# Layer 0: the selection matrix first in its step, and sets 0 to 2 in five steps per two pairs instead of six

## The chip, the cores and the metric

The kernel runs on one core of a Trainium2 chip. Its time is the device time of one execution in microseconds (us); a profiled execution also gives a trace of all engines: PE (matmuls), PEld (its weight loads), DVE (vector), ACT (scalar, activations), POOL (GpSimd) and SP, whose queue issues most transfers.

## The reference

Four graph layers follow one another, each as `x = layernorm(x + layer(x, adj))`, over 128 graphs of 64 nodes with 128 features; all is float32. The change lies in the first, which is a continuous filter: for each of the 64 x 64 possible edges of a graph a distance d is spread over 20 Gaussians, run through a two-layer filter, weighed by a cutoff and summed over the neighbours.

```python
coeff = -0.5 / (widths * widths)
f_ij = jnp.exp(coeff * diff * diff)                 # diff = d_ij - offsets, 20 of them
rcut = 0.5 * (jnp.cos(d_ij * (math.pi / CUTOFF)) + 1.0) * (d_ij < CUTOFF)
y = x @ w_in2f
W = ssp(f_ij @ fw1 + fb1) @ fw2 + fb2               # ssp(v) = softplus(v) - log 2
W = W * rcut[..., None]
agg = jnp.einsum('bjf,bijf->bif', y, W)
out = ssp(agg @ ow1 + ob1) @ ow2 + ob2
```

The second layer is of the same kind with 64 Gaussians; the third and fourth are graph convolutions with the normalized adjacency.

## The kernel before

**Slots.** About a quarter of the edges are there, so the kernel does not compute 64 x 64 of them. A compaction picks the edges of each graph and stores them in DRAM as slots: a distance (d), the neighbour's number (j) and a weight (w). Graphs are sorted by size and taken in pairs, 64 pairs a layer; eight pairs form a set, and all pairs of a set have the same number of slots per graph (`GSLOTS`: 1080, 1092, 1044, 1020, 1008, 1008, 996, 948 in layer 0). Pair n of the loop runs over both layers, 0 to 127.

**Steps.** Two pairs (n and n + 1, n even) are cut into steps. `chunks_of` gives the cuts: in layer 1 wide cuts of 2/5 of a pair, whose two narrow middle ones `steps_of` joins into one step that holds the end of one pair and the start of the next (five steps); in layer 0 two cuts a pair up to 1024 slots (sets 3 to 7, four steps per two pairs) and three above (sets 0 to 2, six steps of 360, 364 or 348 columns). A step works on both graphs of a pair at once.

**What a step is.** The loop over `steps` writes out the order of all engines by hand, and nothing reorders it. With c the step, c1 and c2 the two before it:

- `sums` (DVE): the reductions over the slots of the previous two pairs' m, line 1931 and 1935, in eight parts; `TURNS[beat]["sums"]` says how many parts in each step
- `early`, `side`, `stores`: compaction of later sets (DVE's Max and index, lines 1259 and 1262; POOL's scatters, line 997; SP's loads of rows, line 1019), so many pieces a step; `early` gives 9 in the first 18 steps
- loads (SP, line 1381) of d for pair n + 2 or n + 3; three buffers hold d, three w, two j
- where a pair starts in the step: its `one_hot` (DVE, line 1822), the selection matrix, which writes w where the slot's neighbour number equals the row and zero elsewhere; also, now and then, work for a group of four pairs
- `filter_in(c)`: px, the first filter matmul (PE, line 1846), then Exp on ACT into h. In layer 0 d lies in three thirds on 20 rows each, so a cut over the border of a third needs a matmul more
- `gather(c1)`: pg, the neighbours' features by the selection matrix (PE, line 1875), copied by ACT into m (two buffers)
- the loads of j and w (SP)
- `softplus(c)`: Ln on ACT; then, at two places per two pairs, a set's sine if one is due (ACT, with a load of function tables before and after)
- `filter_out(c2)`: pw, the second filter matmul (PE, line 1861), then `message(c2)`: DVE multiplies pw into m (line 1901)
- `gaussians`: Square and Exp on d of a coming pair (ACT, line 957)

px, pg and pw have one PSUM buffer each. `slot(nodes)` and `slot(befores)` put the work per group of four pairs in between (u, o, back, xT, y, zT, zs on PE).

`TURNS` holds these counts by the number of steps per two pairs (6, 4 and 5, the last for layer 1), `BEFORES` the steps in which `befores` runs.

Of the kernel before, what the change touches and what calls it, by code (L numbers as in the profile page):

```python
# [66 lines left out]

def chunks_of(layer, size):

    if layer == 1:  # L70
        wide = -(-2 * size // 5)
        return (wide, wide, size - 2 * wide, size - 2 * wide, wide, wide)
    n = 2 if size <= 1024 else 3
    return (size // n,) * (2 * n)
# [538 lines left out]
def sparse_stack(ctx: ExitStack, tc: tile.TileContext, t: dict, out: bass.AP, flag):  # L613
# [801 lines left out]
    side, again0, sines = deque(), [], deque()  # L1415
# [400 lines left out]
    def one_hot(n):  # L1816

        _, j, wt = slot_data[n]
        layer, p = pair_at(n)
        size = GSLOTS[layer][p // 8]  # L1820
        hots[n] = wt
        nc.vector.scalar_tensor_tensor(  # L1822
            hots[n][:, 0:size], j[:, 0:size], near, wt[:, 0:size], ALU.is_equal, ALU.mult
        )
# [118 lines left out]
    befores, nodes, convs, sums = deque(), deque(), (deque(), deque(), deque()), deque()  # L1943
# [5 lines left out]
    messages, aggs, phase = {}, {}, [0]  # L1949
# [20 lines left out]
    N = 2 * NP  # L1970
# [12 lines left out]
    early = deque([gathering()])  # L1983
# [33 lines left out]
    def steps_of(n):  # L2017


        layer, p = pair_at(n)  # L2020
        size = GSLOTS[layer][p // 8]
        cuts, at = [], 0
        for m in CHUNKS[layer][p // 8]:
            cuts.append([part_of(n + at // size, at % size, at % size + m)])
            at += m
        if layer == 1:
            cuts[2:4] = [cuts[2] + cuts[3]]
        for k, cut in enumerate(cuts):
            yield dict(
                id=f"{n}_{k}", layer=layer, w=layers[layer], n=n, k=k, beat=len(cuts), parts=cut,  # L2030
                phase=k + p // 2 % 2 * len(cuts),
                size=sum(x["cols"][1] - x["cols"][0] for x in cut),
                starts=[x["n"] for x in cut if x["cols"][0] == 0],
            )
# [12 lines left out]
            late=(2, None, None, 3, None, None), load=(2, None, None, 3, None, None),  # L2047
            gauss=((1, 0), (1, 1), None, (2, 0), (2, 1), None),
            end=(7,) * 6,
        ),  # L2050
        4: dict(
            sums=(2, 3, 2, 2), early=(6, 7, 6, 7), side=(2, 3) * 2,
            late=(2, None, 3, None), load=(2, None, 3, None),
# [10 lines left out]
    FREE, MORE, ONCE, FAST = 4, 4, 1, (0, 0)  # L2064
    SUMS = (2, 2, 3, 4, 4)
    EARLY = {N - gap: q for gap, q in zip((14, 11, 8), small_groups)}
    BEFORES = {6: (3, 4, 7, 8, 9), 4: (2, 3, 5, 6, 7), 5: (7, 8, 9)}

    block = nc.cur_bb.bb.instructions
    past = [None] * 2  # L2070
# [1 line left out]
    for i in range(len(steps) + 2):  # L2072
        c, c1, c2 = steps[i] if i < len(steps) else None, *past
        now = c or dict(steps[-1], k=i - len(steps), phase=i - len(steps), starts=[])
        n, k, beat, layer = now["n"], now["k"], now["beat"], now["layer"]
        turn = {name: values[k] for name, values in TURNS[beat].items()}
        phase[0], at_step[0] = now["phase"] if n < N - FREE else None, i

        if n >= N - 2:
            run(sums, SUMS[k] if c is not None else 9)  # L2080
        else:
            run(sums, turn["sums"])
        run(early, 9 if i < 18 else turn["early" if n < NP - 8 else "end"])
        for _ in range(turn["side"] // 2):
            run(side, min(2, len(side)))
        if turn["side"] % 2:
            run(side, min(1, len(side)))
        run(stores, 1)
        if NP + 5 in now["starts"]:
            assert not early and not side and not convs[0], "edges are still to be gathered"  # L2090
            compacting.close()
            rings.append(ctx.enter_context(tc.tile_pool(name="srings", bufs=4)))
            for q in (0, 1, *small_groups):
                group = GROUPS[1][q]
                blocks[q] = rings[0].tile(
                    [P, group.stop - group.start, P], F32, name=f"blocks{q}", bufs=1
                )
                nc.gpsimd.memset(blocks[q], 0.0)

            small[2] = by_pair(node.tile([P, GS * P], F32, tag="zt", name="small2", bufs=1))  # L2100
            small[3] = zblk
        if c is not None:
            if turn["load"] is not None and n + turn["load"] < N:
                m = n + turn["load"]
                if len(c["parts"]) == 1:
                    slot_data[m], late_loads[m] = later_loads(m)
            for part_ in c["parts"]:
                m, (_, q) = part_["n"], part_["at"]
                if part_["cols"][0] > 0:
                    continue  # L2110
                if m + GS < N:
                    ahead(m)
                if part_["s"] == min(1, len(range(NP)[GROUPS[layer][q]]) - 1):
                    load_nodes(layer, q)
                if m > 0:
                    one_hot(m)
                if m in EARLY:
                    last[EARLY[m]].append(normals_of(EARLY[m]))
            filter_in(c)
            if len(c["parts"]) == 2 and n + 3 < N:  # L2120
                slot_data[n + 3], late_loads[n + 3] = later_loads(n + 3)
        if c1 is not None:
            gather(c1)
        if c is not None and turn["late"] is not None and n + turn["late"] < N:
            late_loads.pop(n + turn["late"])()
        if layer == 1 and befores and (n >= N - 8 or phase[0] in BEFORES[beat]):
            slot(befores)
        if c is not None:
            softplus(c)
            if beat % 2 == 0 and k % (beat // 2) == beat // 2 - 1 and sines:  # L2130

                sines.popleft()()
        if layer == 0:
            slot(nodes)
            if befores and phase[0] in BEFORES[beat]:
                slot(befores)
        if n >= N - MORE:
            slot(nodes)
            if not ONCE:
                slot(convs[2])  # L2140
        if N - FAST[0] <= n < N - FAST[1]:
            slot(convs[1])
        if c2 is not None:
            filter_out(c2)
        for queue in last.values():
            slot(queue)
        if layer == 1:
            slot(nodes)
        if c2 is not None:
            message(c2)  # L2150
        if convs[0]:
            slot(convs[0])
        if n >= N - MORE:
            slot(convs[2])
        if c is not None and turn["gauss"] is not None:
            m, stage = n + turn["gauss"][0], turn["gauss"][1]
            for stage in range(begun.get(m, 0), stage + 1 if m < N else 0):
                gaussians(m, stage)
                begun[m] = stage + 1
        slot(convs[1])  # L2160
        for queue in last.values():
            slot(queue)
        past = [c, c1]
# [70 lines left out]
```

## Time and profile before

| | us |
|---|---|
| median of 3 runs | 1550.03 |
| lowest and highest | 1546.11, 1555.68 |
| the profiled execution | 1555.04 |
| its span | 1553.2 |

The mean granted clock of PE was 0.986. Where the span goes, by the shapes of ACT's Exp in the timeline: sets 0 to 2 of layer 0 from 69.7 to 339.8 us, sets 3 to 7 to 726 us, layer 1 with the two convolutions behind that. What each step takes from one Exp to the next is some 2.7 to 3.7 us in sets 0 to 2 where nothing else comes between, and 4.0 to 4.7 in sets 3 to 7.

A line of the profile names an engine, a line of the program, an operation, what is written from what, the shape and how many there are; after a bar come the busy time and the mean of one in ns, and after another the idle time of the engine before them and what ended it.

### The profile page before, as it was taken

To read this page: it belongs to the slowest core of one execution; us is meant where nothing else is said; L and a number is where in the kernel's file an instruction comes from. 1 tells how busy PE (TensorE), PEld (TensorE's weight loads), DVE (VectorE), ACT (ScalarE), POOL (GpSimd) and SP (SyncE) were. 2 spreads that over 40 slices of the span, in tenths; PEclk is the share of its full clock that TensorE was granted. 3 is DMA by queue.
4 is the path that set the end of the run, shared out by engine and by line. 5 is a ranking of instruction groups with operands and counts; after the bars stand their busy time and mean duration, and the time that the engine had idled before them with its cause. 6 is when DMAs were issued, how large, how long until landed. Compare 5 with 4: busy or idle time off the path is not lost.

```text
span 1553.2 us, 23194 instructions
## 1 busy us (share of the span) xinstructions
PE 1418.0 (91%) x6841; PEld 786.0 (51%) x6841; DVE 1320.7 (85%) x2919; ACT 1316.4 (85%) x1659; POOL 730.6 (47%) x1139
## 2 busy tenths in 40 slices
PE   1388999999989999999999999999999999999975
PEld 1144455544444444555444555555555555555454
DVE  8798889888989899878888888888888888888886
ACT  1368798989888989989999999999999999999853
POOL 2433445545574545424822235554456555464422
PEclk9999999999999999999999999999999999999997
DMA  6856454656554645446666556555555555555201
GB/s 208 260 129 147 115 133 117 138 129 137 134 130 125 146 126 124 125 126 147 155 161 157 135 121 152 132 140 129 135 146 132 135 138 133 120 140 140 65 1 30
DMA packets 122280, 205.60 MB, mean 132 GB/s; under 512 B 47956, under 2 KB 80034, under 8 KB 121506
## 3 DMA queue, kind: packets, MB, share of 16 engines
q1 hardware_dynamic: 113330, 188.40, 49.3%
q0 software_dynamic: 6576, 14.99, 2.9%
q8 instruction: 57, 0.93, 0.3%
q10 hardware_dynamic: 2240, 0.65, 0.2%
q14 instruction: 77, 0.63, 0.1%
HBM read 185.29 MB, written 18.64 MB: 131 GB/s over the span
## 4 chain that ended last, share of the span: by engine, by line
PE 62%; DVE 12%; ACT 10%; DMA 5%; issue 4%; SPq 3%; POOL 0%; DVEq 0%; ACTq 0%
PE pw L1861 23%; PE px L1846 13%; PE pg L1875 11%; ACT h L957 4%; DVE m L1901 3%; SPq L1381 2%; DMA w<-w_dram 2%; PE y L1507 2%; DVE agg L1931 2%; DVE w L1822 1%; PE o L1648 1%; PE hw L1738 1%; PE u L1631 1%; PE back L1657 1%; ACT d L957 1%
## 5 line engine op out<-in xcount | busy, mean ns | idle before, releaser
L957 ACT ACTIVATE h<-h,half 128x1008 f32<-128x1008 f32 (+12 forms) x313 | 332.7, 1063 | 0.1
L957 ACT ACTIVATE m<-pg 128x1008 f32<-128x1008 f32 (+12 forms) x313 | 291.9, 933 | 42.1 <-DVE agg L1935 20.6
L1875 PE MATMUL pg<-w,ys 64*128 64x504 f32 (+15 forms) x1376 | 298.5, 517 | 21.7 <-issue 7.4
L1861 PE MATMUL pw<-h,w_L_gnn_W2T 128*128 128x504 f32 (+8 forms) x640 | 296.8, 586 | 1.8 <-DVE m L1901 1.5
L1931 DVE TENSOR_REDUCE agg<-m 128x32 f32<-128x544 f32 (+14 forms) x455 | 287.3, 669 | 1.8 <-PE u L1631 0.4
L1901 DVE SCALAR_TENSOR_TENSOR m<-pw,c_L_gnn_b,m 128x1008 f32<-128x1008 f32 (+8 forms) x161 | 194.8, 1210 | 106.3 <-PE pw L1861 92.8
L1861 PE MATMUL pw<-h,w_L_gnn_fw 128*128 128x504 f32 (+6 forms) x608 | 252.8, 538 | 8.4 <-DVE m L1901 6.3
L1901 DVE SCALAR_TENSOR_TENSOR m<-pw,c_L_gnn_fb,m 128x1008 f32<-128x1008 f32 (+6 forms) x152 | 168.9, 1111 | 70.1 <-PE pw L1861 51.9
L957 ACT ACTIVATE h<-px,c_L_gnn_b 128x1008 f32<-128x1008 f32 (+8 forms) x160 | 171.5, 1072 | 28.0 <-PE px L1846 27.9
L1822 DVE SCALAR_TENSOR_TENSOR w<-j,row,w 128x1212 f32<-128x1212 bf16 (+12 forms) x128 | 182.4, 1425 | 6.0 <-DMA w<-w_dram 6.0
L957 ACT ACTIVATE h<-px,c_L_gnn_fb 128x1008 f32<-128x1008 f32 (+6 forms) x152 | 148.2, 975 | 45.6 <-PE px L1846 39.2
L1875 PEld LDWEIGHTS pg<-w,ys 64*128 64x128 f32 x1376 | 128.0, 187 | 112.7 <-issue 52.5
L1861 PEld LDWEIGHTS pw<-h,w_L_gnn_W2T 128*128 128x128 f32 x640 | 108.7, 189 | 150.0 <-issue 79.1
L1846 PE MATMUL px<-d,fw 64*128 64x168 f32 (+10 forms) x928 | 154.0, 437 | 25.6 <-ACT d L957 18.7
L1846 PE MATMUL px<-d,w1t 64*128 64x504 f32 (+11 forms) x768 | 172.7, 540 | 0.5 <-ACT h L957 0.4
L1861 PEld LDWEIGHTS pw<-h,w_L_gnn_fw 128*128 128x128 f32 x608 | 105.0, 193 | 90.1 <-issue 43.3
L1846 PEld LDWEIGHTS px<-d,fw 64*128 64x128 f32 x928 | 73.6, 187 | 125.5 <-ACT h L957 33.1
L1476 POOL TENSOR_SCALAR rs<-mv 128x4 f32<-128x4 f32 x55 | 13.9, 253 | 251.4 <-DVE mv L1469 250.4
L957 ACT ACTIVATE d<-d,neg_off 128x1212 f32<-128x1212 f32 (+12 forms) x128 | 120.8, 944 | 9.0 <-DMA d<-d_dram 9.0
L997 POOL DMA_INDIRECT rows<-comb,goes x64 | 72.4, 1131 | 91.8 <-DMA rows<-comb,goes 68.1
L997 POOL DMA_INDIRECT out_dram<-gz,at_row x56 | 72.9, 1302 | 76.2 <-DMA out_dram<-gz,at_row 51.0
L1482 POOL TENSOR_SCALAR x_all<-ny,mv,rs 128x128 f32<-128x128 f32 x120 | 106.3, 894 | 3.2
(333 smaller groups left out, 2280.4 us busy)
## 6 DMA issues: line engine op xcount, KB each, us to landing
d<-d_dram SPq DMA_DIRECT2D x32, 315.0 KB
w<-w_dram SPq DMA_DIRECT2D x32, 315.0 KB
d<-d_dram SPq DMA_DIRECT2D x32, 303.0 KB
w<-w_dram SPq DMA_DIRECT2D x32, 303.0 KB
w<-w_dram SPq DMA_DIRECT2D x32, 252.0 KB
j<-j_dram SPq DMA_DIRECT2D x32, 157.5 KB
j<-j_dram SPq DMA_DIRECT2D x32, 151.5 KB
d<-d_dram SPq DMA_DIRECT2D x16, 300.0 KB
```

The source lines that it names most:

```text
L957: latest = nc.scalar.activation(out_, in_, func, **kw)
L997: nc.gpsimd.indirect_dma_start(out=into, out_offset=bass.IndirectOffsetOnAxis(ap=at, axis=0), in_=rows, in_offset=None,)
L1381: engine.dma_start(to, dram_ap(slots[layer, name][s], first, [[0, to.shape[0]], [1, n]]))
L1482: (nc.gpsimd if apart else nc.vector).tensor_scalar(dst[:, s, :], y[:, s, :], mv[:, s, 0:1], rstd[:, s : s + 1], ALU.subtract, ALU.mult,)
L1507: nc.tensor.matmul(ps[:, s, :], lhsT=xt[:, s * P : (s + 1) * P], rhs=w["win"], start=True, stop=True)
L1631: nc.tensor.matmul(by[:, s, :], lhsT=w["o1"], rhs=of, start=layer == 1, stop=True)
L1822: nc.vector.scalar_tensor_tensor(hots[n][:, 0:size], j[:, 0:size], near, wt[:, 0:size], ALU.is_equal, ALU.mult)
L1846: nc.tensor.matmul(ps[:, b, at : at + m], lhsT=w["w1"][rows, :] if c["layer"] else w["w1"][rows, k, :], rhs=d[rows, col : col + m], start= ...
L1861: nc.tensor.matmul(c["pw"][:, b, :], lhsT=c["w"]["w2"], rhs=c["h"][:, b, :], start=True, stop=True)
L1875: nc.tensor.matmul(ps[:, b, to], lhsT=y[rows, :], rhs=hots[part_["n"]][rows, first:stop], start=True, stop=True,)
L1901: nc.vector.scalar_tensor_tensor(to, c["pw"][:, :, of], c["w"]["b2"], to, ALU.add, ALU.mult)
L1931: nc.vector.tensor_reduce(av[:, :, :, r], both, AX.X, ALU.add)
```

## The change

`chunks_of` cuts layer 0's sets above 1024 slots as layer 1's, and `steps_of` joins the middle cuts wherever there are six. Two pairs of sets 0, 1 and 2 are then five steps of 432, 437 or 436, 418 or 416 columns. They get counts of their own, `TURNS[3]` and `BEFORES[3]`. In all of layer 0 `one_hot` moves from behind the sums and the compaction to the start of the step. The places of the sine are written anew: steps 2 and 4 of five (2 and 5 of six before), 1 and 3 of four as before.

```diff
-    if layer == 1:
+    if layer == 1 or size > 1024:
         wide = -(-2 * size // 5)
         return (wide, wide, size - 2 * wide, size - 2 * wide, wide, wide)
...
-        if layer == 1:
+        if len(cuts) == 6 and (True):
             cuts[2:4] = [cuts[2] + cuts[3]]
...
+        3: dict(
+            sums=(2, 2, 1, 2, 2), early=(5, 6, 5, 6, 6), side=(2, 2, 3, 2, 3),
+            late=(2, None, None, 3, None), load=(2, None, 3, None, None),
+            gauss=((1, 1), None, (2, 0), (2, 1), (3, 0)),
+            end=(7,) * 5,
+        ),
...
-    BEFORES = {6: (3, 4, 7, 8, 9), 4: (2, 3, 5, 6, 7), 5: (7, 8, 9)}
+    BEFORES = {6: (3, 4, 7, 8, 9), 4: (2, 3, 5, 6, 7), 5: (7, 8, 9), 3: (3, 4, 6, 7, 8)}
...
-        turn = {name: values[k] for name, values in TURNS[beat].items()}
+        turns = TURNS[3 if layer == 0 and beat == 5 else beat]
+        turn = {name: values[k] for name, values in turns.items()}
         phase[0], at_step[0] = now["phase"] if n < N - FREE else None, i
 
+        for m in now["starts"] if layer == 0 else ():
+            if m > 0:
+                one_hot(m)
         if n >= N - 2:
             run(sums, SUMS[k] if c is not None else 9)
...
-                if m > 0:
+                if m > 0 and layer == 1:
                     one_hot(m)
...
-            if beat % 2 == 0 and k % (beat // 2) == beat // 2 - 1 and sines:
+            if layer == 0 and k in (beat // 2 - (beat != 5), beat - 1) and sines:
```

For the counts of before: six steps had `sums=(1, 1, 2, 1, 2, 2)`, `early` 2, 5, 5, 2, 5, 5, `side` 2 in each, d of pairs n + 2 and n + 3 loaded in steps 0 and 3, j and w likewise, and the Gaussians as (pair, stage) (1, 0), (1, 1), none, (2, 0), (2, 1), none.

More of the change, by code (lines that the diff above doesn't have):

```diff
@@ L2125, in sparse_stack @@
             late_loads.pop(n + turn["late"])()
-        if layer == 1 and befores and (n >= N - 8 or phase[0] in BEFORES[beat]):
+        if layer == 1 and befores and (n >= N - 8 or phase[0] in BEFORES[3 if layer == 0 and beat == 5 else beat]):
             slot(befores)
@@ L2134, in sparse_stack @@
             slot(nodes)
-            if befores and phase[0] in BEFORES[beat]:
+            if befores and phase[0] in BEFORES[3 if layer == 0 and beat == 5 else beat]:
                 slot(befores)
```

## The prediction

> **What bounds the kernel now.** I read the page first: busy shares, then the chain of work that ended last.
>
> ```profile
> PE 1418.0 (91%) x6841; PEld 786.0 (51%) x6841; DVE 1320.7 (85%) x2919; ACT 1316.4 (85%) x1659; POOL 730.6 (47%) x1139
> PE 62%; DVE 12%; ACT 10%; DMA 5%; issue 4%; SPq 3%; POOL 0%; DVEq 0%; ACTq 0%
> ```
>
> PE leads with 91% and carries 62% of the chain; DVE and ACT stand just behind, and 8% is transfers and their queue. An average says little of a change to one stage, so next come the windows by stage. The shapes of ACT's Exp (h<-px) give the limits: sets 0 to 2 (720, 728, 696 elements, that is two halves of 360, 364, 348 columns) run from 69.7 to 339.8 us, the rest of layer 0 (four wide steps) to 726. "Double pair" below means two pairs, as the step loop takes them: 12 of them lie in sets 0 to 2.
>
> ```profile
> 164.00:339.80 175.80, 165.00 (x808) 90.67 (x804) 152.59 (x404) 151.09 (x219) 93.27 (x146) 0.99 0.54 128
> 339.80:579.90 240.10, 224.92 (x1090) 115.57 (x1088) 218.17 (x608) 207.24 (x255) 133.06 (x225) 0.99 0.54 131
> 579.90:726.00 146.10, 144.59 (x743) 77.28 (x740) 122.90 (x226) 133.45 (x167) 55.36 (x96) 1.00 0.53 132
> ```
>
> Columns: length, then busy time of PE, PEld, DVE, ACT, POOL, the granted clock, DMA share, GB/s. Sets 1 and 2 (8 double pairs, six steps each): 22.0 us per double pair, PE idle 10.8 us or 1.35 each. Sets 3 to 5 (12, four steps): 20.0 us, PE idle 15.2 or 1.27 each. Sets 6 and 7, with little compaction left: idle 1.5 in all, 0.19 each. So PE sets the pace everywhere, its idle time goes with the compaction on DVE, POOL and SP, and hardly with the number of steps.
>
> Then PE's timeline, one undisturbed step of each kind:
>
> ```profile
> 215.62 0.88 PE L1846 MATMUL px<-d,fw 64*128 64x364 f32 x4
> 216.33 0.78 PE L1875 MATMUL pg<-w,ys 64*128 64x364 f32 x4
> 217.04 1.49 PE L1861 MATMUL pw<-h,w_L_gnn_fw 128*128 128x364 f32 x4
> 218.46 0.88 PE L1846 MATMUL px<-d,fw 64*128 64x364 f32 x4
> ...
> 517.26 1.12 PE L1846 MATMUL px<-d,fw 64*128 64x336 f32 x8
> 518.21 1.01 PE L1875 MATMUL pg<-w,ys 64*128 64x504 f32 x4
> 519.16 1.96 PE L1861 MATMUL pw<-h,w_L_gnn_fw 128*128 128x504 f32 x4
> 521.04 1.12 PE L1846 MATMUL px<-d,fw 64*128 64x168 f32 x8
> ```
>
> From px to the next px: 2.84 us at 364 columns, 3.78 at 504. Slope (3.78 - 2.84) / 140 = 6.7 ns a column; what no column explains is 2.84 - 364 x 0.0067 = 0.40 us a step.
>
> **The change part by part.** *One step less per double pair, on PE.* The columns stay (2160, 2184, 2088), the 0.40 goes once: 12 x 0.40 = -4.8 us. The stage rows check it: PE's busy time per double pair is 20.6 against 18.7 us; of the 1.9 the 112 columns explain 0.75, the other 1.1 is two steps, 0.57 each, so -6.8. I take -4.8, the row of steps that are like those changed.
>
> *More pieces in the first matmul.* Cuts of 432 no longer fall on the thirds of 360: 10 pieces per double pair in place of 6, two of them 72 wide (73 and 70 in sets 1 and 2). The 336+168 step above takes 0.95 from px to pg, as long as the 504 pg behind it (0.95), so pieces down to 168 are free. For 72 the bounds are 0.84 ns a column (0.306 us from one 364-wide record to the next), 0.061, and the nearest row, the 128-wide matmuls, 0.111 apart: 0 to 0.05 each, two passes, two pieces, 12 times, so 0 to +2.4 us. I take +2.4. [...]
>
> *ACT and DVE.* Each step has an Exp, a copy and a Ln on ACT:
>
> ```profile
> L957 ACT ACTIVATE h<-h,half 128x728 f32<-128x728 f32 x24 | 21.7, 902 | 0.0
> L957 ACT ACTIVATE h<-px,c_L_gnn_fb 128x728 f32<-128x728 f32 x24 | 20.8, 867 | 7.7 <-PE px L1846 7.6
> L957 ACT ACTIVATE m<-pg 128x728 f32<-128x728 f32 x24 | 18.6, 773 | 3.0 <-PE pg L1875 2.7 <-issue 0.2
> ...
> L957 ACT ACTIVATE h<-h,half 128x1008 f32<-128x1008 f32 x32 | 36.3, 1133 | 0.0
> L957 ACT ACTIVATE h<-px,c_L_gnn_fb 128x1008 f32<-128x1008 f32 x32 | 35.0, 1092 | 10.0 <-PE px L1846 9.4 <-issue 0.4
> L957 ACT ACTIVATE m<-pg 128x1008 f32<-128x1008 f32 x31 | 31.2, 1006 | 12.6 <-DVE agg L1935 5.1 <-PE pg L1875 4.1 <-issue 3.4
> ```
>
> Lines through the two sizes leave fixed parts of 0.30, 0.28 and 0.17: 0.75 us a step, 9.0 in all. DVE's message (971 ns at 728, 1261 at 1008) leaves 0.22, 2.6 in all. ACT idles 24.7 of 175.8 us, waiting mostly for PE, so these are hidden behind PE but for their shares of the chain (10% and 12%): -0.9 and -0.3. [...]
>
> *A tighter wait.* The sums of a double pair are eight parts. With six steps (1, 1, 2, 1, 2, 2) the last is done in step 0 of the double pair after next, with five (2, 2, 1, 2, 2) in step 1, the very step in which ACT's copy reuses that m buffer and, every second time, PE starts u. Four-step sets stand so already: ACT waited there for agg L1935 11.7 us in 20 double pairs, 0.58 each. 12 x 0.58 = 7 us of ACT, which its 24.7 us of idle covers; behind the waiting copy are Ln and the next Exp, and PE after those. At nothing; +7 if the cover is gone.
>
> *Compaction earlier.* A double pair now advances it by 28 pieces in place of 24 (by 45 in place of 54 in the first 18 steps, 9 each). In the order of instructions 250 of its DVE instructions, not 229, lie in the first 12 double pairs; at about 0.25 us (0.21 to 0.29 for Max and index) 5 us are moved ahead and missing later. DVE idles 23 us in each of the two stages: nothing. The sine (0.41 us and two table loads of 1.28) comes once a set as before.
>
> *Loads.* d is read two steps after its load, not three (2 x 4.35 = 8.7 us for 3 x 3.65 = 10.9), j and w of a second pair four, not six (17.4 for 22). The tightest pair I found:
>
> ```profile
> 264.90 2.31 SPq L1381 DMA_DIRECT2D d<-d_dram  x6
> 271.40 0.60 SPq L1381 DMA_DIRECT2D w<-w_dram  x1
> 274.74 0.58 ACT L957 ACTIVATE d<-d,neg_off 128x348 f32<-128x348 f32 x1
> 284.20 1.30 DVE L1822 SCALAR_TENSOR_TENSOR w<-j,row,w 128x1044 f32<-128x1044 bf16 x1
> ...
> 108.01 4.96 DMA w<-w_dram
> ```
>
> d has 7.5 us from the last issue to its use, 5.3 after the change; the chain shows landings of 1.9 and 3.2. It holds.
>
> *The selection matrix first (all of layer 0).* One DVE instruction of 1.3 us and no DMA of its own: it passes the sums, the compaction's DVE part (some 2.5 us), and in program order the work that issues SP's row loads and POOL's scatters, whose own queues it is not in. The message behind all of it waits for the same total. Gain: SP's next load of j waits for it (9.7 us of SP waits from 60 to 345 us), and SP is let go some 2.5 us sooner, off the path: nothing. Loss: it now stands at the head of DVE's queue and waits there for w, with sums, compaction and the message behind it, and PE's pw behind that. For the pair shown, 12.2 us from issue to use shrink by 4.6 and 2.5 to 5.1, against 4.4 to 5.1 of landing in the chain: just in time. At the start it is tighter (pair 2: issue ends 90.8, use 97.1; 3.8 left), about 1 us twice, and ACT, which idled 6.9 us there for d of pair 2, has one piece less of 144 columns done by then, 1 us, less what overlaps: +0.5 to +3, taken as +1.
>
> Sum: -4.8 + 2.4 - 0.9 - 0.3 + 1 = -2.6; with the other row for a step (-6.8) -4.6. I take -3.5: the profiled execution, 1555.04 (span 1553.2), becomes 1551.5. It lies 5.0 above the median of the three runs, so on the median's scale 1550.0 - 3.5 = 1546.5 us.
>
> **The rivals.** *Faster:* what idles PE is the wait for DVE and SP, and the early matrix and longer steps take it away. If the 12 double pairs fell from 1.35 to the 0.19 of sets 6 and 7: 14 us more, 1532.5. For: SP's longest waits are for this instruction. Against: four-step sets under compaction idle the same 1.27.
>
> *Slower:* the matrix at the head of DVE waits for w. It decides once a landing takes over about 5 us. Were it 7 to 7.5, 2 to 2.5 us in each of the 12 second pairs, DVE stops and PE within a step: +24 to +30, so 1571 to 1576. For: margins of 5 us, and landings of 5 at 60 to 125 us. Against: DVE has not waited for w since the first pair (idle before it 6.0 us, once), and the DMA share is 0.54.
>
> *Nothing:* the sums' wait and the pieces eat the gain: -4.8 + 2.4 + part of 7, 1550 to 1554.
>
> **How the numbers follow.** Forecast 0.55, nothing 0.22, faster 0.12, slower 0.11. Runs of before spread 0.6%, so 1% is about what a measurement tells from no change: below 1534.5 or above 1565.5. The forecast's own range is 1540 to 1552 (steps -6.8 or -4.8, pieces 0 or 2.4, start up to +3, run noise of 2 or 3). For 8 in 10 it takes in the nothing case and the near ends of both others, 1534 to 1559. Faster 0.12, same 0.77, slower 0.11.
>
> **What would show it.** Exp shapes of 864, 874 or 872 and 836 or 832, sixty in all; PE's plain step at 432 near 3.30 us; the stage of sets 0 to 2 some 3 us shorter, about 267; ACT's copy waiting for agg L1935 in it, which it does not now; no idle time before L1822. I am wrong if L1822 waits for w in more than the first pairs, if px with a 72-wide piece takes over 0.2 us longer than the pg behind it, or if sets 3 to 7, where the matrix alone moved, change by over 3 us.

## The result and the profile after

The changed kernel takes 1554.97 us in the median of 20 runs (1547.57 to 1558.09), the kernel before 1550.11 in 20 runs beside it: a ratio of 1.0027 [1.0016, 1.0038], or +4.2 us. The forecast was -3.5 us. The time lies within the range that was given, but the sign is wrong. The profiled execution took 1556.62 us, its span 1554.8. That of before is one of its kernel's longer runs (1555.04), so the two spans differ by 1.6 us only, and what the profiles say of a stage is good to some 4 us (two profiles of one order differ by as much, see below). All differences of whole kernels below are ratios times 1550 us, and 0.001 is 1.55 us. A difference between two runs is that of their two ratios, its interval the root of the sum of their squared half-widths.

The page of the kernel after, busy shares and the chain:

```profile
PE 1412.3 (91%) x6985; PEld 794.6 (51%) x6985; DVE 1311.8 (84%) x2907; ACT 1310.3 (84%) x1623; POOL 722.2 (46%) x1139
PE 57%; DVE 13%; ACT 12%; issue 4%; DMA 4%; SPq 3%; POOL 1%; ACTq 0%; DVEq 0%; POOLq 0%
```

PE works 5.7 us less than before, but by the stages below only 1.9 of it in sets 0 to 2, where the steps are fewer, and 3.6 in sets 3 to 7, where the steps are as before. The chain leaves PE (62% before, 57% now) for DVE and ACT. The stages are those of the prediction, each between the same Exps as before (columns: length, then busy time of PE, PEld, DVE, ACT, POOL, the granted clock, DMA share, GB/s). First all of sets 0 to 2, of the kernel before and of the kernel after:

```profile
69.70:339.70 270.00, 245.90 (x1163) 132.80 (x1165) 235.75 (x665) 223.35 (x321) 125.81 (x191) 0.99 0.56 132
```

```profile
70.10:348.60 278.50, 244.01 (x1295) 139.71 (x1297) 236.91 (x696) 217.85 (x286) 129.57 (x210) 0.96 0.54 128
```

Then sets 1 and 2, sets 3 to 5, sets 6 and 7, as in the prediction's windows, after:

```profile
168.90:348.60 179.70, 164.63 (x898) 95.37 (x898) 156.72 (x438) 146.66 (x194) 99.64 (x165) 0.97 0.54 126
348.60:585.70 237.10, 224.51 (x1112) 117.58 (x1110) 216.09 (x591) 209.86 (x257) 130.57 (x229) 1.00 0.53 135
585.70:731.50 145.80, 141.37 (x729) 76.00 (x727) 120.88 (x214) 130.42 (x165) 54.60 (x83) 1.00 0.53 131
```

Sets 0 to 2 take 8.5 us more (270.0 to 278.5), sets 3 to 7 take 3.6 less (386.5 to 382.9), and layer 1 with all behind it takes 3.7 less (827.0 to 823.3). In sets 0 to 2 PE is busy 1.9 us less and idle 10.4 us more (24.1 to 34.5), DVE does 31 instructions more, and the clock falls from 0.99 to 0.96. The step itself is as forecast. PE's timeline:

```profile
217.01 1.63 PE L1861 MATMUL pw<-h,w_L_gnn_fw 128*128 128x437 f32 x4
218.57 1.01 PE L1846 MATMUL px<-d,fw 64*128 64x291 f32 x8
219.41 0.90 PE L1875 MATMUL pg<-w,ys 64*128 64x437 f32 x4
220.24 1.73 PE L1861 MATMUL pw<-h,w_L_gnn_fw 128*128 128x437 f32 x4
```

From pw to pw 3.23 us, against 0.40 + 437 x 0.0067 = 3.33 by the prediction's line. Of ACT's groups in sets 1 and 2:

```profile
L957 ACT ACTIVATE h<-px,c_L_gnn_fb 128x874 f32<-128x874 f32 x16 | 15.8, 990 | 11.2 <-PE px L1846 9.9 <-issue 1.3
L957 ACT ACTIVATE h<-px,c_L_gnn_fb 128x836 f32<-128x836 f32 x16 | 15.3, 959 | 12.4 <-PE px L1846 10.6 <-issue 1.6
L957 ACT ACTIVATE m<-pg 128x874 f32<-128x874 f32 x16 | 14.3, 894 | 2.8 <-DVE agg L1935 2.8
```

And of the page's groups:

```profile
L957 ACT ACTIVATE m<-pg 128x1008 f32<-128x1008 f32 (+11 forms) x301 | 289.9, 964 | 35.1 <-DVE agg L1935 31.4
...
L1875 PE MATMUL pg<-w,ys 64*128 64x504 f32 (+15 forms) x1376 | 293.7, 514 | 0.0
...
L1822 DVE SCALAR_TENSOR_TENSOR w<-j,row,w 128x1212 f32<-128x1212 bf16 (+12 forms) x128 | 176.2, 1376 | 6.0 <-DMA w<-w_dram 6.0
```

ACT's copy waits for the sums, as forecast, and the matrix never waits for w beyond the first pair, as forecast. The line between them was not forecast. The same line before was

```profile
L1875 PE MATMUL pg<-w,ys 64*128 64x504 f32 (+15 forms) x1376 | 298.5, 517 | 21.7 <-issue 7.4
```

so pg's idle time, 21.7 us, is gone, and still the kernel is slower. Something worth more was added.

### The profile page after: what moved, and what is told of

Read it like the earlier page. It is cut to its first block, busy times and chain, and to the rows that moved or that the text cites. A ratio compares the mean times of both kernels' runs of the same rounds, so it can differ in the third digit from the quotient of the medians.

```text
span 1554.8 us, 23416 instructions
## 1 busy us (share of the span) xinstructions
PE 1412.3 (91%) x6985; PEld 794.6 (51%) x6985; DVE 1311.8 (84%) x2907; ACT 1310.3 (84%) x1623; POOL 722.2 (46%) x1139
## 4 chain that ended last, share of the span: by engine, by line
PE 57%; DVE 13%; ACT 12%; issue 4%; DMA 4%; SPq 3%; POOL 1%; ACTq 0%; DVEq 0%; POOLq 0%
PE pw L1861 21%; PE px L1846 12%; PE pg L1875 9%; ACT h L957 6%; DVE m L1901 3%; DVE agg L1931 3%; SPq L1381 2%; DVE w L1822 2%; DMA w<-w_dram 2%; ACT d L957 2%; ACT m L957 2%; PE y L1507 1%; PE back L1657 1%; PE hw L1738 1%; PE o L1648 1%
## 5 line engine op out<-in xcount | busy, mean ns | idle before, releaser
L957 ACT ACTIVATE m<-pg 128x1008 f32<-128x1008 f32 (+11 forms) x301 | 289.9, 964 | 35.1 <-DVE agg L1935 31.4
L1875 PE MATMUL pg<-w,ys 64*128 64x504 f32 (+15 forms) x1376 | 293.7, 514 | 0.0
L1861 PE MATMUL pw<-h,w_L_gnn_fw 128*128 128x504 f32 (+8 forms) x560 | 251.3, 571 | 18.5 <-DVE m L1901 16.6
L1901 DVE SCALAR_TENSOR_TENSOR m<-pw,c_L_gnn_fb,m 128x1008 f32<-128x1008 f32 (+8 forms) x140 | 166.0, 1186 | 69.8 <-PE pw L1861 49.9
L957 ACT ACTIVATE h<-px,c_L_gnn_fb 128x1008 f32<-128x1008 f32 (+8 forms) x140 | 145.2, 1037 | 59.9 <-PE px L1846 44.6
L1846 PE MATMUL px<-d,fw 64*128 64x168 f32 (+22 forms) x1120 | 155.6, 397 | 36.1 <-ACT d L957 18.3
L1822 DVE SCALAR_TENSOR_TENSOR w<-j,row,w 128x1212 f32<-128x1212 bf16 (+12 forms) x128 | 176.2, 1376 | 6.0 <-DMA w<-w_dram 6.0
L1846 PEld LDWEIGHTS px<-d,fw 64*128 64x128 f32 x1120 | 91.5, 191 | 141.8 <-issue 42.2
L1861 PEld LDWEIGHTS pw<-h,w_L_gnn_fw 128*128 128x128 f32 x560 | 96.7, 193 | 103.2 <-issue 65.1
L997 POOL DMA_INDIRECT rows<-comb,goes x64 | 67.3, 1052 | 110.8 <-DMA rows<-comb,goes 81.5
```

Of the source, the lines that this page charges most:

```text
L957: latest = nc.scalar.activation(out_, in_, func, **kw)
L997: nc.gpsimd.indirect_dma_start(out=into, out_offset=bass.IndirectOffsetOnAxis(ap=at, axis=0), in_=rows, in_offset=None,)
L1822: nc.vector.scalar_tensor_tensor(hots[n][:, 0:size], j[:, 0:size], near, wt[:, 0:size], ALU.is_equal, ALU.mult)
L1846: nc.tensor.matmul(ps[:, b, at : at + m], lhsT=w["w1"][rows, :] if c["layer"] else w["w1"][rows, k, :], rhs=d[rows, col : col + m], start= ...
L1861: nc.tensor.matmul(c["pw"][:, b, :], lhsT=c["w"]["w2"], rhs=c["h"][:, b, :], start=True, stop=True)
L1875: nc.tensor.matmul(ps[:, b, to], lhsT=y[rows, :], rhs=hots[part_["n"]][rows, first:stop], start=True, stop=True,)
```

## The experiments

All ran five rounds beside the kernel before. "Six steps" is the kernel before with only the matrix moved; "at 24" or "at 28" is the number of compaction pieces per double pair in sets 0 to 2. The table holds all times; what they mean follows by question.

| kernel | median us | ratio to before, 95% |
|---|---|---|
| matrix first, six steps | 1540.59 | 0.9937 [0.9917, 0.9956] |
| matrix at its old place, five steps | 1559.42 | 1.0046 [1.0029, 1.0062] |
| the change, sums earlier | 1553.15 | 1.0019 [1.0000, 1.0039] |
| the change, Gaussians later | 1556.85 | 1.0048 [1.0030, 1.0066] |
| the change, compaction at 24 | 1549.65 | 0.9995 [0.9978, 1.0012] |
| the change, all repairs and Gaussians later | 1551.16 | 1.0011 [1.0000, 1.0022] |
| six steps, more pieces | 1549.89 | 1.0003 [0.9991, 1.0015] |
| six steps, late sums | 1542.76 | 0.9953 [0.9935, 0.9971] |
| six steps, compaction at 28 | 1560.43 | 1.0055 [1.0039, 1.0071] |
| five steps, three repairs | 1547.62 | 0.9974 [0.9962, 0.9986] |
| the same, no narrow pieces | 1549.23 | 0.9985 [0.9972, 0.9998] |
| six steps, matrix first in layer 1 too | 1548.26 | 0.9967 [0.9952, 0.9982] |
| before, compaction at 28 | 1561.80 | 1.0103 [1.0087, 1.0119] |
| six steps, compaction at 22, then 27 | 1539.15 | 0.9945 [0.9932, 0.9958] |
| five steps, three repairs, light starts | 1540.25 | 0.9947 [0.9932, 0.9962] |
| the change, light starts | 1551.73 | 1.0028 [1.0018, 1.0038] |
| six steps, 36 spare Max | 1549.06 | 0.9981 [0.9966, 0.9995] |
| light starts, matrix at its old place | 1550.23 | 0.9991 [0.9977, 1.0005] |

### One half of the change at a time

The matrix first alone, in six steps:

```diff
+        for m in now["starts"] if layer == 0 else ():
+            if m > 0:
+                one_hot(m)
         if n >= N - 2:
...
-                if m > 0:
+                if m > 0 and layer == 1:
                     one_hot(m)
```

> Only the selection matrix is moved to the start of its step in layer 0; sets 0 to 2 keep six steps. Theory W (the loss is single waits that the five steps and their counts bring: d of pair 2 at the start, DVE's wait for POOL line 1282, the sums in the step that needs them): the move does nothing by itself or gains a little, -3 to +1 us against before. Theory M (the loss comes from the matrix at the head of DVE's queue): +3 to +6 us. Sign: under M, L1822 shows idle time before it, under W none beyond the first pair's 6 us.

Five steps alone are the changed kernel without this edit.

> Five steps with their counts, the matrix at its old place behind sums and compaction. Theory W: the waits stay, +2 to +7 us against before. Theory M: -3 to +1 us.

Measured: the matrix alone gives -9.8 us [-12.9, -6.8], which neither theory had; five steps alone cost +7.1 [+4.5, +9.6]. So the change is a gain and a loss. They do not simply add: -9.8 and +7.1 make -2.7, and the change measures +4.2. In the five steps as they stand in the change, the same move of the matrix is worth only -3.0 us (within 3.1). Where the gain comes from, one pair start shows. The timeline of before:

```profile
82.74 0.88 PE L1846 MATMUL px<-d,fw 64*128 64x360 f32 x4
82.77 2.31 DVE L1253 TENSOR_TENSOR ad<-same,ad 128x512 f32<-128x512 f32 x1
...
84.99 1.33 DVE L1822 SCALAR_TENSOR_TENSOR w<-j,row,w 128x1080 f32<-128x1080 bf16 x1
...
86.25 0.96 DVE L1901 SCALAR_TENSOR_TENSOR m<-pw,c_L_gnn_fb,m 128x720 f32<-128x720 f32 x1
...
86.43 1.03 PE L1875 MATMUL pg<-w,ys 64*128 64x360 f32 x4 [2.81 <-issue]
```

Columns are start, duration, engine and instruction; in brackets the idle time before it and who ended it. The matrix ends at 84.99 + 1.33 = 86.32, pg starts 0.11 later: it had waited 2.81 us for the matrix, which stood behind a 2.31 us compaction instruction. The profile names "issue" and not DVE. Of 22 such gaps of pg over 0.15 us in the trace of before, 21 (20.3 of 21.4 us) end 0.06 to 0.11 us after a matrix does, 18 us of it in layer 0. The same place with the matrix first, six steps:

```profile
80.09 1.33 DVE L1822 SCALAR_TENSOR_TENSOR w<-j,row,w 128x1080 f32<-128x1080 bf16 x1
...
82.35 0.77 PE L1875 MATMUL pg<-w,ys 64*128 64x360 f32 x4
...
82.91 2.31 DVE L1253 TENSOR_TENSOR ad<-same,ad 128x512 f32<-128x512 f32 x1
...
85.15 0.95 DVE L1901 SCALAR_TENSOR_TENSOR m<-pw,c_L_gnn_fb,m 128x720 f32<-128x720 f32 x1
...
86.03 1.09 DVE L1259 MAX8 comb<-ad 128x8 f32<-128x64 f32 x8
...
86.16 2.77 PE L1861 MATMUL pw<-h,w_L_gnn_fw 128*128 128x360 f32 x4 [1.95 <-DVE m L1901]
```

pg does not wait. The compaction instruction now holds up the message instead, and pw behind it: 1.95 us of the 2.81 come back as another wait. Over sets 0 to 2 PE's wait for the message grows from 4.4 us in before to 9.3, which is one reason why 18 us of waiting are worth about 10. In the two profiles sets 0 to 2 fall by 4.5 us (270.0 to 265.5) and sets 3 to 7 by 7.4 (386.5 to 379.1).

### The late sums, the Gaussians

```diff
-            sums=(2, 2, 1, 2, 2), early=(5, 6, 5, 6, 6), side=(2, 2, 3, 2, 3),
+            sums=(2, 1, 2, 2, 2), early=(5, 6, 5, 6, 6), side=(2, 2, 3, 2, 3),
```

> The changed kernel with sums (2, 1, 2, 2, 2) in place of (2, 2, 1, 2, 2) for the five-step sets, so that the last of the eight parts is done in step 0 and not in step 1, where ACT's copy needs the buffer. In the changed kernel ACT waited 8.3 us for agg L1935 in sets 0 to 2, before nothing. If that wait is on the path, 2 to 5 us less than the changed kernel (-1 to +2 against before) and no wait of m for agg there; if ACT's idle time covers it, as I had it, within 1 us of the changed kernel (+3 to +5), the wait gone all the same.

The other way round, six steps with the matrix first and the sums late, as the change has them:

```diff
-            sums=(1, 1, 2, 1, 2, 2), early
+            sums=(1, 2, 1, 1, 2, 2), early
```

> Six steps with the matrix first and sums (1, 2, 1, 1, 2, 2) in place of (1, 1, 2, 1, 2, 2), which leaves the last of the eight parts to step 1, as the five steps do. If that wait is on the path: +2 to +6 us above the matrix-first kernel, and ACT's m waiting for agg L1935 in sets 0 to 2; if ACT's idle time covers it: within 1 us.

Measured: -1.2 us (within 3.5 either way) for the one, +2.5 (within 4.1) for the other. ACT's waits for agg L1935 in sets 0 to 2 were none before, 8.3 us after. Neither difference is clear of nothing, and the first leaves at most 4.7 of the 8.3 us on the path; so most of it is covered.

The Gaussians of the changed kernel, a step later in the double pair:

```diff
-            gauss=((1, 1), None, (2, 0), (2, 1), (3, 0)),
+            gauss=((1, 1), None, None, (2, 0), (2, 1)),
```

> The changed kernel with Square and Exp of coming pairs one step later in the five-step sets, gauss ((1, 1), none, none, (2, 0), (2, 1)), so that d is read three steps after its load again. In the changed kernel ACT idled 10.0 us for d of pair 2 at the start, 6.9 before. If the shorter lead costs there, set 0 gets 2 to 4 us shorter and the kernel as much; if the start is bound by SP's queue whatever waits for it, within 1 us of the changed kernel.

It costs 3.3 us (within 3.3) where a gain was possible. In its profile the first double pair is 3.1 us shorter than in the change (26.4 against 29.5), as the expectation had it for the start; what the start gains is lost elsewhere, and the runs do not show where.

### The compaction's pace in five steps

```diff
-            sums=(2, 2, 1, 2, 2), early=(5, 6, 5, 6, 6), side=(2, 2, 3, 2, 3),
+            sums=(2, 2, 1, 2, 2), early=(5, 5, 4, 5, 5), side=(2, 2, 3, 2, 3),
```

> The changed kernel with 24 compaction pieces per two pairs in sets 0 to 2, as before, in place of 28. Theory W: DVE's wait of 7.9 us for POOL L1282 comes of compaction running into the scatters of the set before; at the old pace it goes or shrinks, sets 0 to 2 get 3 to 8 us shorter, and sets 3 to 7 give back what compaction is left over, 1 to 3: -1 to -4 against the changed kernel, 0 to +3 against before. Rival (the alignment of POOL's work is an accident, not a matter of pace): the wait stays or another of its size stands elsewhere, within 2 us of the changed kernel.

-5.0 us (within 3.1) against the changed kernel. What it takes away can be seen in the trace of after, in time:

```profile
282.21 1.13 POOL L997 DMA_INDIRECT rows<-comb,goes  x1 [0.17 <-issue]
...
288.06 1.01 POOL L997 DMA_INDIRECT rows<-comb,goes  x1 [4.27 <-DMA rows<-comb,goes]
...
289.10 0.71 POOL L1282 TENSOR_TENSOR same<-comb 128x312 f32<-128x312 f32 x1
...
289.85 1.53 DVE L1287 SCALAR_TENSOR_TENSOR same<-same 128x312 f32<-128x312 f32 x1 [7.92 <-POOL same L1282]
...
291.31 0.58 DVE L1582 TENSOR_SCALAR zblk<-zr 64x256 f32<-64x256 f32 x2
...
291.94 1.11 PE L1586 MATMUL zT<-ident,zblk 128*128 128x128 f32 x4 [4.95 <-DVE zblk L1582]
```

POOL's scatter waits 4.27 us for the transfer of the one before it, DVE 7.92 for what stands behind the scatter on POOL, and PE 4.95 for DVE. Between the two instructions, lines 1282 and 1287, the program leaves a pause of four pieces (`wait_steps`), and a step of six pieces can hold it whole. That this pause was what had kept them apart is argued from the listing. The wait is in the trace of all five kernels with five steps at 28 (7.9 us after, 7.2 with the matrix at its old place, 10.1 with earlier sums, 8.6 with light starts, 1.2 with later Gaussians) and in none at 24; in six steps at 28, five pieces a step at the most, it is not either. The kernels with light starts at 24 have steps of six pieces too and no such wait, so six pieces in a step do not bring it by themselves.

All repairs at once, with the sine moved away from its place ahead of zt (PE zs had waited 2.6 us for that once in after) to steps 0 and 4:

```diff
-            sums=(2, 2, 1, 2, 2), early=(5, 6, 5, 6, 6), side=(2, 2, 3, 2, 3),
+            sums=(2, 1, 2, 2, 2), early=(5, 5, 4, 5, 5), side=(2, 2, 3, 2, 3),
...
-            gauss=((1, 1), None, (2, 0), (2, 1), (3, 0)),
+            gauss=((1, 1), None, None, (2, 0), (2, 1)),
...
-            if layer == 0 and k in (beat // 2 - (beat != 5), beat - 1) and sines:
+            if layer == 0 and k in ((0, 4) if beat == 5 else (beat // 2 - 1, beat - 1)) and sines:
```

> Five steps with the matrix first and four repairs: sums (2, 1, 2, 2, 2), Gaussians one step later, 24 compaction pieces per two pairs, and the sine's places at steps 0 and 4, where no zt is due. Theory W (the loss of the five steps is single waits, each tied to a count): it comes to the time of the matrix-first kernel with six steps or below it, 1536 to 1543 us. Rival P (five steps are slower in themselves: more pieces on PE, each wait of a longer step dearer): it stays 5 us or more above, 1546 to 1552.

It gave back 2.5 us only, and the next kernel, the same with the Gaussians left as in the change, says why: those had cost 5.7 (within 2.5). These are the "three repairs".

> The changed kernel with three of its placements put back (last sums in the first step, compaction at 24 pieces, sine in steps 0 and 4) and the Gaussians as in the change. If five steps lost only by such waits, 1541 to 1545, level with six steps and the matrix first. If the five steps cost something in themselves (pieces, longer turns through DVE and ACT), 1547 to 1551, with PE's busy time in sets 1 and 2 still about 160 to 162 us and its idle time spread over many small gaps.

-8.2 us against the change (within 2.5), yet 5.7 (within 3.5) above six steps with the matrix first. By the ratio that is 1546.0, between the two expectations: the waits are more than half of the loss, not all.

### Pieces of the first matmul

Six steps with ten pieces per double pair instead of six, four of them 72 wide:

```diff
                 end = min(stop, (k + 1) * third)
+                if c["layer"] == 0 and c["beat"] == 6 and c["k"] in (0, 1, 4, 5) and first % third == 0:
+                    end = first + third // 5
```

> Six steps with the matrix first, and in four of the six steps px cut at a fifth of a third (72, 288), so that a double pair has ten pieces, four of them about 72 wide. Read from the changed kernel's trace (0.89 from px to pg with a 73-wide piece, 0.84 with a 146-wide one) a narrow piece costs 0.05 us: 12 x 4 x 0.05 = 2.4 us above the matrix-first kernel (+1 to +3.5). If the pieces are what makes five steps slow: +7 or more.

Five steps with none under 116 wide:

```diff
-        wide = -(-2 * size // 5)
+        wide = -(-2 * size // 5) if layer == 1 else 4 * size // 9
```

> The kernel with three repairs, but the cuts of sets 0 to 2 at 4/9 of a pair instead of 2/5: steps of 480, 480, 240, 480, 480 columns, pieces of 360 and 120, 240 and 240, 120 and 120; the same number of pieces, none narrower than 116. If the 72-wide pieces cost (0.10 us a step on PE), it is 1 to 5 us below the kernel with three repairs. If narrow pieces are free, it is level with it or up to 4 us above, since the steps are less even.

The two do not agree. The first costs 10.2 us (within 3.6), the second gains nothing (+1.7, within 2.7). In the first, PE's busy time in sets 0 to 2 rises from 244.6 to 250.1, 5.5 us for 48 narrow pieces in two passes, 0.057 each, about the upper bound that the prediction took (up to 1.7 of the 5.5 can be lost clock, 8.5 us there against 6.8). PE's idle time there rises by another 3.6 (20.9 to 24.5); why, stays open. In the change there are 24 such pieces, so some 2.7 us of PE by this price, an estimate; PE's busy time falls in spite of them, as the last five-step kernel below shows. No kernel with five steps and six pieces was run, so what ten pieces cost there is not measured.

### The pace by itself

Six steps, matrix first, at the changed kernel's pace, and the kernel before at it:

```diff
-            sums=(1, 1, 2, 1, 2, 2), early=(PACE - 2, PACE + 1, PACE + 1) * 2, side=(2,) * 6,
+            sums=(1, 1, 2, 1, 2, 2), early=(4, 5, 5) * 2, side=(2,) * 6,
```

> The fast version so far (six steps, matrix first) with the compaction of sets 0 to 2 at the changed kernel's pace: 28 pieces per double pair instead of 24. If the pace by itself costs what the slower pace gave back in five steps (-5 us), the time is 3 to 6 us above that version, near 1544 to 1547, and the trace has a wait of DVE for a POOL scatter (L1282) of several us. If the pace hurt only together with five steps, the time stays within 2 us of it, 1539 to 1543, and no such wait appears.

> The kernel before, matrix at its old place, with 28 compaction pieces per double pair instead of 24 in sets 0 to 2. If the pace costs by DVE's total (about 6 us of DVE work moved ahead into stages where DVE is 91% busy beside PE), it costs here too: 6 to 18 us above before, ratio 1.004 to 1.012. If it costs only because the early matrix stands in the same step, the ratio is within 0.002 of 1.

Measured: +18.3 us (within 3.9) and +16.0 [+13.5, +18.4]. Nothing of the change is in the second one but the pace. The cost is there without five steps and without the early matrix, and it is at least three times what was expected of the first. (DVE is busy 235.75 of 270.0 us in sets 0 to 2 of before, 87%; the 91% of the second expectation is PE's.) In both the four added pieces stand in the steps in which a pair starts, two in each, so that pace and place change together. At 28 the place was varied in five steps only, where it made no difference (below). By PE's waits in sets 0 to 2 (engine and line, what it waited for: us in all, times, the longest), six steps with the matrix first at 24:

```profile
PE pw L1861 <- DVE m L1901: 9.3, 9, 2.0
PE px L1846 <- ACT h L957: 4.3, 4, 2.0
```

and at 28:

```profile
PE pw L1861 <- DVE m L1901: 16.9, 15, 2.5
PE zs L1594 <- ACT zt L957: 4.7, 3, 3.9
PE px L1846 <- ACT h L957: 4.5, 3, 1.9
```

Sets 0 to 2 of these two profiles differ by as much as the medians, 18.3 us (265.5 to 283.8), and 15.1 of it is PE's idle time. The message comes later, and more compaction stands ahead of it on DVE: pw waits 7.6 us more. And once a wait of 3.9 us is new: the sine with its two table loads, due at another moment, stood on ACT ahead of zt (from 200.16 to 203.16 us), and PE's zs behind that. At 28 sets 0 to 2 have 6 us more of DVE's compaction in them, by the two traces (87.7 against 81.8 us, lines 1252 to 1287). The 16.0 us of the second kernel can't be placed so: its profile is the shortest of its runs, that of before a long one, and sets 0 to 2 differ by 7.8 us in them (270.0 to 277.9).

What part of it is DVE's own time, I tried with work that sets nothing going:

```diff
         run(early, 9 if i < 18 else turn["early" if n < NP - 8 else "end"])
+        if layer == 0 and beat == 6 and i >= 18 and c is not None and k % 3 == 0:
+            for _ in range(2):
+                nc.vector.max(out=spare_top, in_=ident[:, 0:A])
```

> Six steps, matrix first, compaction as before (24 pieces per double pair), with two more Max instructions of DVE on a constant (64 values a partition, some 0.21 us each) in each step where a pair starts, from the fourth double pair to the twelfth: 36 in all, 7.7 us of DVE work, no DMA and nothing for POOL or SP. They add work whose result is not used. If the faster compaction cost 18 us by DVE's time alone, this costs 12 to 20 us over six steps with the matrix first: ratio 1.001 to 1.007. If it cost through POOL's scatters, SP's loads or their transfers, this costs 0 to 7 us: ratio 0.993 to 0.998.

The 36 instructions, as the trace's answer for that tile has them:

```profile
L2090 DVE MAX8 spare_top<-ident x36: 201/225/229, 145.6 to 331.3; 128x8 f32<-128x64 f32 x36
```

36 x 0.225 = 8.1 us of DVE cost 6.8 us (within 3.8), at the upper edge of the second expectation. So DVE's time in these stages is not free, and may cost its full length, although DVE idles there (29.7 us in sets 0 to 2 of six steps with the matrix first): of the 15.6 us of it in sets 1 and 2, 11.9 are waits for pw, and the added work stands behind such a wait and ahead of the next message. At that rate the 6 us of moved compaction cost 5; the rest of the 18, some 13 (within 5), is not DVE's length. The traces show single collisions that the pace sets off, as that of the sine; how the rest divides among them, POOL's scatters and the transfers stays open.

Less compaction in sets 0 to 2, more later (diff against six steps with the matrix first):

```diff
+            sums=(1, 1, 2, 1, 2, 2), early=(2, 4, 5) * 2, side=(2,) * 6,
...
+            sums=(2, 3, 2, 2), early=(7, 7, 6, 7), side=(2, 3) * 2,
```

> Six steps, matrix first, 22 pieces per double pair in sets 0 to 2 instead of 24, and 27 instead of 26 in sets 3 to 7 until the compaction is done. If the cost goes with the total of DVE work in sets 0 to 2 (18 us for 4 pieces per double pair), sets 0 to 2 are 4 to 9 us shorter than with 24, and sets 3 to 5 up to 5 us longer: ratio 0.989 to 0.994. If 24 lies below the point from which the pace costs, the ratio is 0.993 to 0.998.

0.9945, level with 24 (+1.2, within 3.6): below 24 nothing is gained.

### Where the pieces lie, and what five steps are worth

Five steps with three repairs, the 24 pieces moved out of the two steps in which a pair starts, and the changed kernel's 28 likewise:

```diff
-            sums=(2, 1, 2, 2, 2), early=(5, 5, 4, 5, 5), side=(2, 2, 3, 2, 3),
+            sums=(2, 1, 2, 2, 2), early=(3, 6, 3, 6, 6), side=(2, 2, 3, 2, 3),
```

> The kernel with three repairs, its 24 pieces placed 3, 6, 3, 6, 6 instead of 5, 5, 4, 5, 5: fewer in the two steps where a pair starts and the matrix stands. If what five steps still lose is the load of these steps, it comes down to six steps with the matrix first: ratio 0.992 to 0.995. If place does not matter, it stays at 0.996 to 0.999.

```diff
-            sums=(2, 2, 1, 2, 2), early=(5, 6, 5, 6, 6), side=(2, 2, 3, 2, 3),
+            sums=(2, 2, 1, 2, 2), early=(3, 7, 4, 7, 7), side=(2, 2, 3, 2, 3),
```

> The changed kernel with its 28 pieces placed 3, 7, 4, 7, 7 instead of 5, 6, 5, 6, 6, all else as changed. If the load of the steps where a pair starts is what costs, 4 to 8 us below the changed kernel: ratio 0.997 to 1.000. If the total costs, as changed: 1.001 to 1.005.

At 24 the place is worth -4.2 us (within 3.0), at 28 nothing (0.2, within 2.3). With 24 and light starts five steps reach 0.9947, level with six steps and the matrix first, and 12.4 us (within 2.9) below the change. That is the price of the change's pace and placements together; the places of the last sums and of the sine are in it, and the sine's was never changed alone.

Last, this kernel with the matrix back at its old place, so that against before only the number of steps differs (and the placements that go with it):

> Five steps with all placements repaired (last sums in the first step, 24 pieces as 3, 6, 3, 6, 6, sine in steps 0 and 4), but the selection matrix at its old place: against the kernel before, five steps for six and nothing else that costs. By the sum of the forecast, without the start: -4.8 + 2.4 - 0.9 - 0.3 = -3.6 us, or -5.6 with the other row for a step: ratio 0.996 to 0.998. If the pieces and the longer turns eat the saved step: 0.999 to 1.003. If the early matrix is worth its 10 us in five steps too, this lies 0.005 to 0.008 above the same kernel with the matrix first.

Ratio 0.9991, -1.4 us [-3.6, +0.8]; and the matrix first is worth -6.8 (within 3.2) in five steps. Its sets 0 to 2, in the columns of the stage rows above:

```profile
70.00:337.70 267.70, 239.72 (x1297) 136.28 (x1297) 230.47 (x655) 218.51 (x287) 123.90 (x190) 0.98 0.55 133
```

267.7 us; the prediction had said "about 267" of the changed kernel. PE's busy time is 6.2 us below before (245.9 to 239.7), but its idle time 3.9 above (24.1 to 28.0).

That growth lies at the start. The first double pair took 25.6 us in before and 30.1 here, with PE idle for 5.0 and 10.4; the eleven others took 244.4 and 237.6, with PE idle for 19.2 and 17.5. What stands at the start can be seen in the change as well. ACT before:

```profile
89.45 0.59 ACT L957 ACTIVATE d<-d,neg_off 128x360 f32<-128x360 f32 x1 [6.88 <-DMA d<-d_dram]
```

ACT and PE in the change:

```profile
90.52 0.59 ACT L957 ACTIVATE d<-d,neg_off 128x360 f32<-128x360 f32 x1 [10.03 <-DMA d<-d_dram]
...
92.03 2.00 PE L1846 MATMUL px<-d,fw 64*128 64x72 f32 x8 [7.40 <-ACT h L957]
```

ACT waits for d of pair 2, and PE for ACT. PE's wait is 6.7 to 7.6 us in each of the nine kernels with five steps and the Gaussians as in the change, and 1.1 at the longest in before. It is the longest single wait of PE in sets 0 to 2 of the change, and with the Gaussians a step later, where the start is shorter, the kernel is slower.

### The matrix first in layer 1 too

```diff
-        for m in now["starts"] if layer == 0 else ():
+        for m in now["starts"]:
...
-                if m > 0 and layer == 1:
-                    one_hot(m)
```

> Six steps, with the selection matrix first in layer 1 too. In the trace of before PE's pg waited just behind a selection matrix 1.58 and 0.55 us in layer 1, so 2 us less than with layer 0 alone, 1537 to 1540. If the early matrix in layer 1 makes DVE wait for w (loads there follow the same rows), it is level or 1 to 5 us above.

0.9967: no gain over layer 0 alone, if anything a loss of 4.7 us (within 3.8). But the order of layer 0 is the same in both, and in the two profiles its sets 0 to 2 took 265.5 and 269.7 us. So single profiles of one order differ by 4 us, and part of this difference may be no more than that.

## Why the prediction was wrong, point by point

The change adds up from three measured parts: five steps -1.4, the matrix first -6.8 (in five steps), the faster compaction with its placements +12.4. The sum is +4.2, as it must be, since each is the step from one kernel to the next. In another order the parts have other sizes: -9.8 for the matrix from before, -3.0 (within 3.1) as the last step to the change.

- *One step less per double pair, with the pieces and the ACT and DVE shares.* Forecast -4.8 + 2.4 - 0.9 - 0.3 = -3.6 us (-5.6 by the other row), measured -1.4 [-3.6, +0.8] with the start in it, for which the forecast had +1 on top. The mechanism was right. By the profiles, the steps gave what was forecast or more (-6.8 us in the eleven double pairs behind the first, good to some 4), and the start took most of it back.
- *A tighter wait.* Appeared as described, on ACT in sets 0 to 2, 8.3 us in all where 7 were reckoned, and was covered for the most part. Right.
- *Compaction earlier.* This is the step that turned the sign: "DVE idles 23 us in each of the two stages: nothing." The amount was of the right order (5 us forecast, about 6 in the traces of six steps, 9.8 between before and the change), but the idle time was no cover. The cost was +16.0 us alone in the kernel before, +18.3 with the matrix first in six steps, and the slower pace alone gave the change 5.0 back. The error was to weigh an engine's idle total against the work that is added. DVE waits for pw, then runs through sums, compaction and message, and PE's next pw waits for that message; work put ahead of the message prolonged the turn, whatever DVE idled elsewhere (in six steps with the matrix first PE's waits for the message were 9.3 us at 24, 16.9 at 28). The spare Max show this for about 5 of the 18 us; the traces show single waits in the rest, and its division stays open. The prediction's own first part held the clue: PE's idle time "goes with the compaction on DVE, POOL and SP". Nothing came back in sets 3 to 7: they took 384.3 to 389.8 us in the four profiles with the matrix at its old place and 378.5 to 383.6 in the sixteen with it first, whatever the pace, so the 3.6 us less are the matrix's. A little came back behind them, where DVE is busy 5.8 us less (689.0 to 683.2): layer 1 with all behind it took 821.7 to 826.0 us in the seven profiles at 28 and 824.8 to 828.9 in the thirteen others. And the price is not linear: 22 pieces were no better than 24.
- *The selection matrix first.* "Gain: ... off the path: nothing", measured -9.8 in six steps, -6.8 in five with the placements put right. The loss was looked for on DVE (a wait for w, which did not come: the Slower rival fell) and on the start, and the gain only on SP. That PE's pg reads the matrix was in the listing, and pg's 21.7 us of idle time in the page of before; they were not put together: the profile gave "issue" as the releaser of 7.4 us of it and ACT of nearly all the rest.
- *The start.* Taken as +1 us of 0.5 to 3. The first double pair took 25.6 us before, 28.6 with the matrix alone, 30.1 with five steps and the matrix at its old place, 29.5 after. So the matrix alone was at the upper end of its range, and the five steps, which read d sooner, cost more than that: with d read a step later, the first double pair took 26.4. This term was too small by some 3 us.
- *Loads.* They held: after, ACT waited for d beyond the start for 1.0 us in all.

The faster rival (a further 14 us from early matrix and longer steps) had half of the mechanism, the matrix; the Nothing case had the right size for the wrong reasons. Two errors of opposite sign kept the time within the range, which is luck. Of the marks named beforehand, sets 3 to 7 changing by over 3 us was the one that showed: they changed by 3.6.

The three fastest kernels are six steps with the matrix first (0.9937), the same with compaction at 22 and 27 (0.9945), and five steps with three repairs and light starts (0.9947). Their intervals overlap; the first is the smallest edit.

## What to carry to other kernels

Here idle time on DVE was no cover for work that stood behind it and ahead of what PE waited for: 8.1 us of spare Max cost 6.8 (within 3.8), where DVE had idled 29.7. So follow one turn of the loop, and see what stands behind the added work in its queue. Where a multiply's input is written by an engine that also does background work, look for its start just after that writer's end (0.06 to 0.11 us in 21 of 22 gaps here), whatever releaser the profile names. And when a loop's steps change number, keep background work constant per unit of time, not per step, before anything else is compared: 28 pieces in place of 24 cost 16.0 and 18.3 us in six steps.

## What the runs showed of the hardware

Behind two gaps on PE the granted clock fell, and the matmuls took longer than their like later on. Windows of after, around the 4.95 us gap shown above (same columns as the stages):

```profile
285.00:290.00 5.00, 2.00 (x14) 1.00 (x12) 0.15 (x1) 4.74 (x7) 1.91 (x3) 1.00 0.69 131
290.00:295.00 5.00, 3.05 (x7) 1.88 (x8) 4.95 (x8) 1.07 (x2) 4.04 (x4) 0.63 1.04 222
295.00:300.00 5.00, 5.00 (x27) 3.25 (x26) 4.93 (x21) 2.04 (x3) 1.97 (x3) 0.69 0.32 78
```

0.37 and 0.31 of 5 us are 3.4 us of clock lost; pw at 293.06 took 3.15 us, the next, of the same shape, at 299.71, 1.57. In the trace of before, after a pg gap of 2.13 us that ended at 178.83:

```profile
175.00:180.00 5.00, 2.87 (x11) 0.82 (x9) 4.96 (x5) 2.61 (x5) 4.50 (x4) 0.92 0.18 43
180.00:185.00 5.00, 5.00 (x23) 3.33 (x21) 2.60 (x9) 3.15 (x5) 4.05 (x8) 0.74 0.71 200
```

0.08 and 0.26 of 5 us: 1.7 us lost; this pg took 1.28 us, the next, at 184.28, 0.78. In windows of 5 us from 70 to 355 the lost clock sums to 3.4 us before, 10.2 after, 11.9 in six steps at 28, 5.1 with light starts at 24: each within 0.1 of a multiple of 1.7. So a part of the price of the added waits, near 7 us of clock at the most between before and after, may be this, an estimate from these sums. It is not what decides: six steps with the matrix first lost 6.8 so, and are the fastest. Which gaps bring it, these traces do not tell: the one of 2.13 us was followed by 1.7 us of lost clock, while behind one of 1.81 us that ended at 111.32 in the same trace the windows from 110 to 120 show 1.00.
